# A transformer block on one core: side work of the attention stage given fixed places, a first output tile inside attention, and two units taking turns in the down projection

## The chip, the cores and the metric

The kernel runs on one core of a Trainium2 chip, in one launch. The metric is the device time of that launch in microseconds (us); several runs are made and their median is compared. A profile of one further execution gives the trace that is read below. "PE" is the matrix engine TensorE, "DVE" VectorE, "ACT" ScalarE, "POOL" GpSimd, and "SP" the sequencer that issues every DMA of this kernel.

## The reference

The block takes 4096 tokens of width 512 in float32: linear attention with 16 heads over 4 key/value heads, a residual and a layer norm, then a gated feed-forward network with Hadamard transforms, a residual and a second layer norm.

```python
q, k, v = x @ Wq.T, x @ Wk.T, x @ Wv.T          # 16 heads, 4 kv heads, head size 128
q, k = rope(q), rope(k)
qf, kf = elu(q) + 1, elu(k) + 1
# a running state over the tokens, per head
state += kf[:, None] * v[None, :];  z += kf
o = (qf @ state) / (qf @ z + 1e-6)
x = layernorm(x + o @ Wo.T)
h = fwht(x * SU_ug) / 64
h = silu(h @ W_gate.T * s_gate) * (h @ W_up.T * s_up)      # 2048 wide
x = layernorm(x + (fwht(h * SU_dp) / 64) @ W_down.T * s_down)
```

## The kernel before, in words

**Arithmetic.** Each float32 operand of a product is split in two parts of the type float32r: the high part is an ACT copy (`hi`), the low part a subtraction on DVE or POOL (`lo`); this is `hilo`, lines 88 to 90. A product is three matmuls: high by high, high by low, low by high.

**Attention** (lines 140 to 507). The key/value heads are worked in two passes of two heads; each pass goes over 16 blocks of 256 tokens. A block has four slots `(n, g, p)`: head `g`, half `p` of the block; 128 slots in all, counted by `i`. In a slot the loop traces a projection of two query heads (`proj_q`, line 314, five slots ahead of its use), parts of the next block's keys, values and state, the scores of the next slot (`scores`, 327, whose result `A` two POOL operations of line 351 mask), and the products of this slot (`av`, 354: `ps_num` and `ps_den`). The numerators go to `num_d` in DRAM; denominators go to `den_d`, and `recip` (107) turns them into reciprocals in `rec_d`.

**Side work of attention.** Weights of the second pass are loaded and split around slot 56. `wcomb` (385) forms sums of the up and gate weights that a Strassen-like product with 7 instead of 8 block products needs later: for each of eight pairs four loads, four POOL additions (line 394) and four stores to `was_d`. `load_wo` (100) loads and splits the output weights `Wo`, 14 heads from slot 118 on.

**Output projection** (624 to 773). For each of 32 token tiles `norm_o` (630) multiplies the numerators (`nt`) by the broadcast reciprocals (`rb`) and splits the result; 48 matmuls of 512 columns make the tile (`ps_wo`, line 737); two tiles are layer-normed together. Beside it run the front transform of the feed-forward input and the Hadamard transform of `W_down` (`prep_down`).

**Up and gate** (843 to 942): 32 steps of 7 products (`ps_a`, `ps_b`, `ps_c`, line 870). **Down** (992 to 1049): eight units of 512 tokens, each with the same 7 products `s` of 48 matmuls (`ps_da`, `ps_db`, `ps_dc`, line 1025). For the first unit the 7 operands of `W_down` are also loaded (`braw`) and split (`split_b`, 797); later units find them there. The activations come as `hraw` and are split by `h_split`.

**What sets the order.** The program is traced in the order of the source and then reordered engine by engine by the framework's list scheduler (`schedule_with_timeline_sim`), within what data and buffers allow; each engine then runs its own list strictly in order. `tc.keep_in_program_order` holds an instruction behind everything traced before it on its engine. All DMAs are one such list, on SP: an entry that waits holds back all that follow. Each DMA also waits for the one eight places before it, so eight are under way at most. Buffers come from rings: `praw` has 3 for raw inputs (tag `raw`), `wres` 28 tiles (24 hold the weights of a pass, so 4 are free), the pool `rp` 10 for `hraw` and `braw`.

Of the kernel before, what the change touches and what calls it, by code (L numbers as in the profile page):

```python
# [26 lines left out]
LAG = 1  # L27
# [16 lines left out]
def kernel(  # L44
# [28 lines left out]
    yq_d = [[dram.tile([128, 2, 512], F32, name=f"yq_d{f}_{k}") for k in range(7)] for f in range(4)]  # L73
    was_d = [{k: dram.tile([128, 512], F32, name=f"was_d{p}{k}") for k in ("S1", "S2", "S3", "S4")} for p in range(8)]
# [7 lines left out]

    def load_raw(src):
        raw = praw.tile([128, 512], F32, tag="raw", name="raw")
        dma(raw, src)
        return raw

    def hilo(hi, lo, src, eng=V):
        S.activation(hi, src, AF.Copy)  # L89
        eng.tensor_tensor(lo, src, hi.bitcast(F32), ALU.subtract)  # L90

    def load_w(src, pool=wres, eng=V, **kw):
        raw = load_raw(src)
        hi, lo = (pool.tile([128, 512], F32R, tag="w", name=n, **kw) for n in ("wh", "wl"))
        hilo(hi, lo, raw, eng)
        return hi, lo

    WO = []

    def load_wo(n):  # L100
        for _ in range(n):
            if len(WO) < NH - 2:
                WO.append(load_w(wo[len(WO)], eng=G if len(WO) % 2 else V))

    late = {}

    def recip(b):
        dn = pout.tile([128, 2, 16], F32, tag="dn", name="dn", bufs=2)
        for j in range(2):
            dma(dn[:, j], den_d[2 * b + j].rearrange("g h c q -> (g h c q)").rearrange("(p n) -> p n", p=128))  # L110
        V.reciprocal(dn, dn)
        for j in range(2):
            dma(rec_d[2 * b + j].rearrange("(p n) -> p n", p=128), dn[:, j])
# [3 lines left out]
    def pre_rb(t, g, pin=False):  # L117
        rb = late["p"].tile([128, 512], F32, tag="rb", name="rb", bufs=5)
        dma(rb, rec_d[t][g * 512:(g + 1) * 512].partition_broadcast(128), pin)
        cur[t]["rb"].append(rb)  # L120

    def pre(t):
        if t in (12, 16):
            recip(NB - 2 + (t == 16))
        nt = late["p"].tile([128, 16, 128], F32, tag="nt", name="nt", bufs=2)
        cur[t] = dict(nt=nt, rb=[])
        if t:
            dma(nt, num_d[t].rearrange("p g n -> p (g n)"), t < 3)
        if t < 2:
            for g in range(4):  # L130
                if t == 0:
                    dma(nt[:, 4 * g:4 * g + 4], num_d[t][:, g])
                pre_rb(t, g, t == 1 and g == 0)
        if t % 2 == 0:
            cur["yp"] = late["p"].tile([128, 2, DM], F32, tag="yp", name="yp", bufs=3)
        cur[t]["yp"] = cur["yp"]
        dma(cur["yp"][:, t % 2], x_n[t * 128:(t + 1) * 128])


    with ExitStack() as es:  # L140
# [18 lines left out]
        def weights_v(s, j):  # L159
            W["v", s, j] = load_w(wv[s, :, j * 512:(j + 1) * 512])  # L160

        def weights_k(s, g):
            W["k", s, g] = load_w(wk[2 * s + g])

        def weights_q(s, g):
            for h in range(4):
                W["q", s, g, h] = load_w(wq[8 * s + 4 * g + h])

        def load_x(n):
            b = n % NB  # L170
            hi = pe.tile([128, 4, 256], F32R, tag="xh", name="xh")
            lo = pe.tile([128, 4, 256], F32R, tag="xl", name="xl")
            hf, lf = (a.rearrange("p k t -> p (k t)") for a in (hi, lo))
            for j in range(2):
                c = slice(j * 512, (j + 1) * 512)
                if n >= NB:
                    dma(hf[:, c], xs_d[b][:, 0, c])
                    dma(lf[:, c], xs_d[b][:, 1, c])
                else:
                    hilo(hf[:, c], lf[:, c], load_raw(x_t[b, :, c]))  # L180
                    dma(xs_d[b][:, 0, c], hf[:, c])
                    dma(xs_d[b][:, 1, c], lf[:, c])
                yield
            csb = pe.tile([128, 2, 256], F32, tag="csb", name="csb")
            dma(csb, cs[b])
            blk[n] = dict(xh=hi, xl=lo, csb=csb)
# [198 lines left out]
        def wcomb(p):  # L385
            r = {}
            for it in range(2):
                for kh in range(2):
                    x = wres.tile([128, 2, 2, 128], F32, tag="w", name="wq")
                    dma(x, wug[2 * p + it].rearrange("p (u k m) -> p u k m", u=2, k=4)[:, :, 2 * kh:2 * kh + 2])  # L390
                    r[it, kh] = x
            for key, o, a, b, op in (("S3", (0, 0), (0, 0), (1, 0), ALU.subtract), ("S1", (1, 0), (1, 0), (1, 1), ALU.add),
                                     ("S2", (1, 1), (0, 0), (1, 1), ALU.subtract), ("S4", (0, 1), (0, 1), (1, 1), ALU.add)):
                G.tensor_tensor(r[o], r[a], r[b], op)
                dma(was_d[p][key], r[o].rearrange("p u k m -> p (u k m)"))
# [3 lines left out]
        NQ = len(slots)  # L399
        gx = load_x(0)  # L400
# [3 lines left out]
        dma(rowm_s, rowm)  # L404
# [3 lines left out]
        dma(idt, ident)  # L408
        dma(sel32, sel)
# [17 lines left out]
        run(load_x(1))  # L427
        run(state(0, 0))
# [6 lines left out]
        nsc = SA  # L435
        gk = gs1 = gv = None
        for i, (n, g, p) in enumerate(slots):
# [11 lines left out]
            if i == NQ - 10:  # L449
                load_wo(NH - 2)  # L450
            if i == NQ - 3:
                early.close()
                late["s"] = ExitStack()
                late["p"] = late["s"].enter_context(tc.tile_pool(name="cl", bufs=2, side="right", reuse_waits="tile"))
                pre(0)
# [44 lines left out]
            if sl == (1, 0) and 18 <= n < 26:  # L500
                wcomb(n - 18)
            if sl == (1, 1):
                if NB + LAG <= n < N - 2 + LAG:
                    recip(n - NB - LAG)
                blk.pop(n - 1, None)

        pre(1)
# [13 lines left out]
    def xtile(shape, dt, name):  # L521
        return mid.tile(list(shape), dt, tag="x4", name=name, bufs=2)
# [101 lines left out]
    with ExitStack() as es:  # L624
        p2 = es.enter_context(tc.tile_pool(name="c2", bufs=2, reuse_waits="tile"))
# [4 lines left out]
        def norm_o(t, g):  # L630
            c = cur[t]
            rb = c["rb"][g].rearrange("p (h n) -> p h n", h=4)
# [10 lines left out]
        load_wo(NH)  # L643
        for h in (NH - 2, NH - 1):
            w = xtile([128, 2, 512], F32R, "wx")
            hilo(w[:, 0], w[:, 1], load_raw(wo[h]))
            WO.append((w[:, 0], w[:, 1]))
        for g in range(KVH):
            norm_o(0, g)
# [77 lines left out]
        for t in range(32):  # L727
            if t + 2 < 32:
                pre(t + 2)
            ps = pwo.tile([128, DM], F32, tag="wo", name="ps_wo")  # L730
            i = 0
            for g in range(KVH):
                oh, ol = cur[t][g]
                for h in range(4):
                    wh, wl = WO[4 * g + h]
                    for l, r in ((oh, wh), (oh, wl), (ol, wh)):
                        T.matmul(ps, l[:, h], r, start=i == 0, stop=i == 47)  # L737
                        i += 1
                if t == 31:
                    for s in (2 * g, 2 * g + 1):  # L740
                        if s < 7:
                            asplit(0, s)
                if t + 1 < 32:
                    norm_o(t + 1, g)
                    if t + 2 < 32:
                        pre_rb(t + 2, g)
            yp = cur[t]["yp"]
            y = yp[:, t % 2]
            V.tensor_tensor(y, ps, y, ALU.add)
# [9 lines left out]
            if t >= 1:  # L759
                step(gd, 4)  # L760
# [16 lines left out]
    rp = ctx.enter_context(tc.tile_pool(name="rp", bufs=10, reuse_waits="tile"))  # L777
    BW = [None] * 7
# [33 lines left out]
    def h_split_x(s, his, los):  # L812
        HOP[0, s] = []
        for qd, raw in enumerate(HR.pop((0, s))):
            hi, lo = (x[qd // 2][:, 2 * (qd % 2):2 * (qd % 2) + 2] for x in (his, los))
            hilo(hi, lo, raw, G if qd == 3 else V)
            HOP[0, s].append((hi, lo))

    with ExitStack() as es:
# [23 lines left out]
        for n in range(NS):  # L843
# [15 lines left out]
            for s, tag in enumerate(SEQ):  # L859
# [41 lines left out]
                if p == 7:  # L901
# [4 lines left out]
                    elif s == 0:  # L906
# [3 lines left out]
                        h_load(0, 1)  # L910
# [6 lines left out]
                    elif s == 4:  # L917
                        split_b(1)
                        h_load(0, 2)
                    elif s == 6:  # L920
                        split_b(2)
                        load_b(3)
# [21 lines left out]
    with ExitStack() as es:  # L944
        pd = es.enter_context(tc.tile_pool(name="d1", bufs=2, reuse_waits="tile"))
        order = [(n, s) for n in range(len(units)) for s in range(7)]
        for n in range(1, len(units)):
# [43 lines left out]
        y_load(0)  # L991
        for idx, (n, s) in enumerate(order):
            if 0 < idx and idx + 1 < len(order):
                h_split(*order[idx + 1])
            if n == 0 and s + 3 < 7:
                split_b(s + 3)
            if 0 < idx and idx + 2 < len(order):
                h_load(*order[idx + 2])
            if n == 0 and s + 4 < 7:
                load_b(s + 4)  # L1000
# [4 lines left out]
            if s == 3 and n + 1 < len(units):  # L1005
                y_load(n + 1)
# [100 lines left out]
```

## Time and profile before

| | |
|---|---|
| median of 3 runs | 2345.06 us (2343.75 to 2345.25) |
| the profiled execution | 2340.29 us, its span 2338.2 us |
| mean granted clock of TensorE | 0.989 |
| PE busy / DVE / ACT / POOL | 2269.3 / 1812.0 / 1401.7 / 1243.7 us |
| moved by DMA | 484.16 MB, mean 207 GB/s |
| attention, first to last product | about 4.8 to 963.6 us |
| output projection | about 966 to 1360 us |
| up and gate / down | about 1360 to 2001 / 1985 to 2338 us |

The span is the time from the first to the last instruction in the trace; the execution's own time is 2.1 us longer. Rows of the timeline give start, duration, engine, source line, operation, tile written and tiles read, and in brackets the idle time of that engine just before, with what ended it. A table of windows gives, for a stretch of the span, each engine's busy time, the clock that was granted to PE, and the share and rate of the DMA engines. Matmuls are pipelined and a matmul's end is modelled, so a matmul that is issued late looks long: the distance between starts says more than the busy share.

### The profile page before, as it was taken

What the parts mean: (1) busy time and instruction counts of PE and PEld (TensorE: products, weight loads), DVE (VectorE), ACT (ScalarE), POOL (GpSimd) and SP (SyncE); (2) the same over time, 40 slices, a digit from 0 to 9 for tenths busy, and PEclk for the clock granted to TensorE, in tenths of its full rate; (3) what the DMA queues carried; (4) which work ended last, traced back from release to release, by engine and by line L of the source; (5) the groups of instructions that cost most, each with busy time, mean ns of one, the idle gap of its engine ahead of it and who ended that gap; (6) DMA issues with size and microseconds to landing.
All of it is one profiled execution on the core that took longest, in us unless ns stands there. A gap on an engine that the chain in (4) does not pass through costs nothing.

```text
span 2338.2 us, 42338 instructions
## 1 busy us (share of the span) xinstructions
PE 2269.3 (97%) x14432; PEld 2015.0 (86%) x14432; DVE 1812.0 (77%) x2812; ACT 1401.7 (60%) x2483; POOL 1243.7 (53%) x999
## 2 busy tenths in 40 slices
PE   7999999988999999899999999999999999899998
PEld 6999999987899999688878887788878888799998
DVE  7999999988898889678898776676766766665555
ACT  6777777766677777344444466655655655555553
POOL 2455454476654445367888526565565555533332
PEclk9999999999999999899999999999999999899999
DMA  6554555677744445878997977775765657867673
GB/s 186 145 152 146 161 161 155 170 214 218 213 133 129 129 135 142 279 256 269 279 294 253 312 240 217 245 254 187 227 207 188 223 189 212 285 229 249 224 248 128
DMA packets 369528, 484.16 MB, mean 207 GB/s; under 512 B 68670, under 2 KB 224384, under 8 KB 365344
## 3 DMA queue, kind: packets, MB, share of 16 engines
q1 hardware_dynamic: 369312, 481.45, 66.0%
q8 instruction: 114, 1.87, 0.3%
q14 instruction: 102, 0.84, 0.1%
HBM read 282.76 MB, written 156.76 MB: 188 GB/s over the span
## 4 chain that ended last, share of the span: by engine, by line
PE 83%; DVE 6%; DMA 5%; issue 2%; POOL 2%; ACT 1%; SPq 1%; DVEq 0%; POOLq 0%; ACTq 0%
PE ps_wo L737 15%; PE ps_a L870 15%; PE ps_qk L244 13%; PE ps_da L1025 8%; PE ps_b L870 7%; PE ps_num L371 5%; PE ps_db L1025 4%; PE ps_c L870 4%; PE ps_s L294 3%; PE ps_v L197 3%; PE ps_dc L1025 2%; PE ps_sc L337 1%; PE ps_sc L338 1%; PE ps_den L372 1%; DVE x L230 1%
## 5 line engine op out<-in xcount | busy, mean ns | idle before, releaser
L351 POOL TENSOR_SCALAR_AFFINE_SELECT A<-A 64x512 fp32r<-64x512 f32 x256 | 220.4, 861 | 286.9 <-DVE am L347 187.5
L244 PE MATMUL ps_qk<-xh,wh 128*128 128x256 f32 x1280 | 358.9, 280 | 6.3 <-DVE x L230 3.7
L244 PE MATMUL ps_qk<-xl,wh 128*128 128x256 f32 x1280 | 356.9, 279 | 0.6 <-DVE xl L90 0.6
L244 PE MATMUL ps_qk<-xh,wl 128*128 128x256 f32 x1280 | 357.1, 279 | 0.0
L90 DVE TENSOR_TENSOR wol<-A,woh 128x512 fp32r<-128x512 f32 x217 | 231.4, 1071 | 106.9 <-ACT woh L89 92.4
L852 POOL TENSOR_TENSOR cc<-cc 128x512 f32<-128x512 f32 x96 | 149.2, 1556 | 278.8 <-ACT cc L849 169.9
L226 POOL TENSOR_TENSOR sw<-sw,csb 128x512 f32<-128x512 f32 x160 | 219.7, 1374 | 141.9 <-ACT sw L225 133.8
L244 PEld LDWEIGHTS ps_qk<-xh,wh 128*128 128x128 f32 x1280 | 242.5, 189 | 8.0 <-DVE x L230 3.3
L244 PEld LDWEIGHTS ps_qk<-xl,wh 128*128 128x128 f32 x1280 | 241.7, 189 | 2.0 <-DVE xl L90 0.8
L244 PEld LDWEIGHTS ps_qk<-xh,wl 128*128 128x128 f32 x1280 | 241.7, 189 | 0.8
L89 ACT ACTIVATE woh<-A 128x512 fp32r<-128x512 f32 x217 | 135.5, 630 | 129.0 <-PE ps_b L870 75.2
L89 ACT ACTIVATE hah<-hraw 128x512 fp32r<-128x512 f32 x216 | 134.8, 630 | 129.5 <-PE ps_da L1025 68.1
L870 PE MATMUL ps_a<-yol,woh 128*128 128x512 f32 x512 | 202.5, 395 | 0.0
L90 POOL TENSOR_TENSOR hal<-hraw,hah 128x512 fp32r<-128x512 f32 x77 | 101.5, 1319 | 189.1 <-PE ps_da L1025 73.1
L870 PE MATMUL ps_a<-yoh,woh 128*128 128x512 f32 x512 | 201.9, 396 | 0.0
L870 PE MATMUL ps_a<-yoh,wol 128*128 128x512 f32 x512 | 199.4, 396 | 0.0
L90 DVE TENSOR_TENSOR hal<-hraw,hah 128x512 fp32r<-128x512 f32 x139 | 102.3, 744 | 111.7 <-PE ps_da L1025 45.7
L737 PE MATMUL ps_wo<-wh,oh 128*128 128x512 f32 x448 | 178.6, 399 | 2.8 <-ACT oh L89 2.8
L737 PE MATMUL ps_wo<-wh,ol 128*128 128x512 f32 x448 | 178.6, 399 | 0.0
L737 PE MATMUL ps_wo<-wl,oh 128*128 128x512 f32 x448 | 178.0, 397 | 0.0
L231 ACT ACTIVATE sw<-x,neg 128x512 f32<-128x512 f32 x160 | 115.5, 722 | 78.0 <-DVE x L230 75.9
L877 ACT ACTIVATE sv<-ps_a,wsc 128x512 f32<-128x512 f32 x192 | 127.2, 680 | 39.6 <-PE ps_a L870 39.5
(256 smaller groups left out, 7290.2 us busy)
## 6 DMA issues: line engine op xcount, KB each, us to landing
hraw<-hop_d SPq DMA_DIRECT2D x224, 256.0 KB
vd<-vhl SPq DMA_DIRECT2D x128, 256.0 KB
num_d<-num SPq DMA_DIRECT2D x128, 256.0 KB
rb<-rec_d SPq DMA_DIRECT2D x128, 256.0 KB
hop_d<-hS SPq DMA_DIRECT2D x128, 256.0 KB
nt<-num_d SPq DMA_DIRECT2D x31, 1024.0 KB
A<-in_wug_dram SPq DMA_DIRECT2D x93, 256.0 KB
hop_d<-cc SPq DMA_DIRECT2D x64, 256.0 KB
```

Source lines behind the costliest of these rows:

```text
L89: S.activation(hi, src, AF.Copy)
L90: eng.tensor_tensor(lo, src, hi.bitcast(F32), ALU.subtract)
L226: G.tensor_tensor(sw, sw, sinb, ALU.mult)
L231: S.activation(sw, x1, AF.Exp, bias=neg1)
L244: T.matmul(ps[:, j], W[key][wa][:, k * 128:(k + 1) * 128], B[xa][:, k], start=i == 0, stop=i == 11)
L351: G.affine_select(ah, ah.bitcast(F32), pattern=[[0, 8], [1, 64]], compare_op=ALU.is_ge, fill=0.0, base=0, channel_multiplier=-1)
L371: T.matmul(ps[:, c2], l, r, start=i == 0, stop=i == len(ops) - 1)
L737: T.matmul(ps, l[:, h], r, start=i == 0, stop=i == 47)
L852: G.tensor_tensor(x, x, c.pop(("g", q)), ALU.mult)
L870: T.matmul(ps, w[:, u, k], y[:, k], start=first and i == 0, stop=i == 5, skip_group_check=not first)
L877: S.activation(x, ps, AF.Copy, scale=sc)
L1025: T.matmul(ps[:, j], ops[qd][al][:, r, js], BW[s][bl][ip], start=first and i == 0, stop=i >= 45 or last and i == 23, skip_group_check=True)
```

## The change

The output weights, the weight sums, the first output tile and the down units change place; no arithmetic is added or removed.

1. At the start the first 14 raw tiles (inputs, `wv`, `wk`, `wq`) are all loaded ahead, into `praw` and into rings that are idle then (`num`, `s32`, `sh`, `sl`); the copies of block 0 to `xs_d` move behind block 1's load. Half of the query weights' low parts go to POOL.
2. `wcomb` becomes a generator whose pieces are pinned to slots 4 to 43 and 62 to 101, one piece in a slot, one POOL addition in two.
3. `Wo` heads 0 to 11 are loaded and split one head a slot in slots 102 to 115, stored to a new `wo_d` in DRAM, and loaded back ready split in slots 121 to 123, when weight tiles come free. Heads 12 to 15 come raw in slot 124 and are split at the end.
4. Output tile 0 is normalised in slots 116 to 126 and multiplied (`ps_w0`) within the attention block, where the scheduler may mix it with the last slots.
5. In the down stage units 0 and 1 take turns, product by product, so that a split operand of `W_down` serves two products in a row.

Reciprocals are computed a block after their load, `rb` and `yp` rings are shared between two pools of the same total, and `prep_down` starts at tile 3 instead of 1.

```diff
     def load_raw(src):
-        raw = praw.tile([128, 512], F32, tag="raw", name="raw")
+        pool, tag = first.pop(0) if first else (praw, "raw")
+        raw = pool.tile([128, 512], F32, tag=tag, name="raw")
         dma(raw, src)
         return raw
...
+    def wo_stage(h):
+        raw = praw.tile([128, 512], F32, tag="raw", name="raw")
+        dma(raw, wo[h], True)
+        yield
+        hi, lo = (wres.tile([128, 512], F32R, tag="w", name=x) for x in ("wh", "wl"))
+        hilo(hi, lo, raw, G if h % 2 else V, True)
+        yield
+        dma(wo_d[h][0], hi, True)
+        dma(wo_d[h][1], lo, True)
+
+    def wo_load(*hs):
+        for h in hs:
+            hi, lo = (wres.tile([128, 512], F32R, tag="w", name=x) for x in ("wh", "wl"))
+            dma(hi, wo_d[h][0], True)
+            dma(lo, wo_d[h][1], True)
+            WO.append((hi, lo))
...
             for key, o, a, b, op in (("S3", (0, 0), (0, 0), (1, 0), ALU.subtract), ...
-                G.tensor_tensor(r[o], r[a], r[b], op)
-                dma(was_d[p][key], r[o].rearrange("p u k m -> p (u k m)"))
+                yield
+                pin(G.tensor_tensor(r[o], r[a], r[b], op))
+                yield
+                dma(was_d[p][key], r[o].rearrange("p u k m -> p (u k m)"), True)
...
+        first.extend([(praw, "raw")] * 3 + [(p3, t) for t in ("num", "s32", "sh", "sl") for _ in range(3)])
...
-            if sl == (1, 0) and 18 <= n < 26:
-                wcomb(n - 18)
+            if 4 <= i < 44 or 62 <= i < 102:
+                go(gw)
+            elif 102 <= i < 116:
+                go(gwo)
+            elif i == 116:
+                o_load(0, *(wres.tile([128, 4, 128], F32R, tag="w", name=x) for x in ("oh0", "ol0")))
...
+            elif i == 121:
+                wo_load(0, 1, 2)
+            elif i == 122:
+                wo_load(3, 4, 5, 6, 7)
+            elif i == 123:
+                wo_load(8, 9, 10, 11)
...
+        o_split(2, V)
+        pre_rb(5)
+        o_split(3, V)
+        wo_split(G, 12, 13)
+        wo_split(V, 14)
+        wo_split(G, 15)
+        ps0 = pmm.tile([128, DM], F32, tag="mm", name="ps_w0")
+        wo_tile(0, ps0)
...
-        order = [(n, s) for n in range(len(units)) for s in range(7)]
-        for n in range(1, len(units)):
+        order = [(n, s) for s in range(7) for n in range(2)]
+        order += [(n, s) for n in range(2, len(units)) for s in range(7)]
+        for n in range(3, len(units)):
             order.remove((n, 0))
             order.insert(order.index((n - 1, 5)), (n, 0))
...
         y_load(0)
+        y_load(1)
         for idx, (n, s) in enumerate(order):
             if 0 < idx and idx + 1 < len(order):
                 h_split(*order[idx + 1])
-            if n == 0 and s + 3 < 7:
-                split_b(s + 3)
+            if n == 0 and s + 2 < 7:
+                split_b(s + 2)
```

## The prediction, made before the changed kernel was run

> **What bounds the kernel now.** I read the page, then a table of windows, then the waits, then timelines at the worst places. PE is busy for 97% of the span and carries 83% of the chain that ended last, so only PE's lost time can be won, and the matmuls stay the same in number. The windows show where it is lost: in the start, in the middle of attention, at the change to the output projection, and at the start of down. In the stretches between, PE is never idle.
>
> ```profile
> PE 83%; DVE 6%; DMA 5%; issue 2%; POOL 2%; ACT 1%; SPq 1%; DVEq 0%; POOLq 0%; ACTq 0%
> ...
> 0.00:60.00 60.00, 44.41 (x300) 41.42 (x301) 42.95 (x64) 35.65 (x59) 16.64 (x20) 0.94 0.59 181
> 400.00:680.00 280.00, 258.81 (x2028) 241.67 (x2027) 243.96 (x389) 188.57 (x337) 172.62 (x153) 0.99 0.65 192
> 932.80:982.10 49.30, 38.01 (x178) 30.20 (x176) 35.26 (x58) 21.78 (x41) 19.15 (x21) 0.79 0.85 264
> 2001.00:2031.00 30.00, 18.95 (x134) 18.45 (x133) 20.36 (x22) 12.67 (x23) 15.88 (x11) 0.77 0.87 285
> ```
>
> Columns are window, length, busy time of PE, its weight loads, DVE, ACT, POOL, then granted clock, DMA share and GB/s. To be seen: the four places, and that the granted clock falls there too. The causes stand in the waits and timelines:
>
> ```profile
> 10.48 5.52 SPq L58 DMA_DIRECT2D raw<-in_wq_dram  x4
> ...
> POOL wq L394 <- DMA wq<-in_wug_dram: 15.1, 8, 5.1
> PE ps_num L371 <- POOL A L351: 11.5, 11, 3.2
> ...
> 475.31 1.26 POOL L394 TENSOR_TENSOR wq<-wq 128x512 f32<-128x512 f32 x1 [5.21 <-issue]
> 477.35 0.51 PE L371 MATMUL ps_num<-A,vd 128*128 128x256 f32 x2 [3.21 <-POOL A L351]
> ...
> 938.61 0.63 ACT L89 ACTIVATE wh<-raw 128x512 fp32r<-128x512 f32 x1 [1.60 <-DMA raw<-in_wo_dram]
> 939.78 0.58 PE L371 MATMUL ps_num<-qh,sh 128*128 128x256 f32 x1 [3.89 <-ACT num L375]
> ...
> 2015.55 0.63 ACT L89 ACTIVATE wdzh<-braw 128x512 fp32r<-128x512 f32 x1 [4.41 <-DMA braw<-wdop_d]
> PE ps_da L1025 <- ACT hah L89: 10.5, 1, 10.5
> ```
>
> At the start, loads of raw weights wait for one of three buffers. In the middle a POOL addition of `wcomb` waits for its load, and the masks behind it in POOL's list, and so PE, wait too. At 938 an ACT copy of `Wo` waits for its DMA, and the copy that empties a PSUM bank stands behind it. In down, ACT waits for `braw` with the activations' copies behind.
>
> **What each place costs now.** A full slot of attention takes 6.975 us (the first `ps_den` of slots 13 and 25 start at 149.7 and 233.4). *Middle:* slots 47 and 85 start so at 386.9 and 683.5: 296.6 us for 38 slots, 265.1 at the full pace, so 31.5 lost, more than the 21.2 of idle, since the matmuls between waits also start late. *Start:* 300 matmuls at 0.118 us (the step between starts at full clock) are 35.4 of 60 us; 4.8 us pass before the first, so 19.8 is lost. *Change of stage:* the last `ps_qk` starts at 932.7 and the first output tile ends at 982.1. The 130 matmuls of attention in between are 15.3 us at 0.118, the tile 48 x 0.233 = 11.2: 22.9 lost. *Down:* from 2001.6 to 2027.4 run two products, 2 x 5.71: 14.4 lost. Together 88.6.
>
> **The change, part by part.**
>
> *Start.* The order of SP's list after the change has the 14 raw loads and `csb` ahead of every store; they no longer wait for buffers, only for the DMA eight places before. PE's gaps of 2.8 us (for `wv`, at 9.78) and 2.6 (for `wq`, at 28.3) go, and four `lo` parts leave DVE (4 x 0.69 = 2.8). What is late next is DVE: it is busy 39.4 of 40 us from 40 to 80. So the gain is what DVE starts earlier and is spared: about 5.4 + 2.8. I take 8; bounds 3 (the 3.9 MB at 220 GB/s come no sooner) and 13.
>
> *Middle.* POOL's list now has one addition per two slots, two slots behind its loads; 1.29 us every 13.95, on an engine busy 152 of 300 us before slot 44 and 113 of 240 after 62. The four loads, and each store, a slot after its addition, fill SP's list in even steps. Nothing of `wcomb` and `Wo` remains between slots 44 and 62. But the second pass's 24 splits stand where they stood (slots 48 and 55 to 58): they keep a loss. Slots 48 to 50 now last 8.4 and 8.8 us instead of 6.975 (3.3 lost); slots 55 to 59 last 42.7 instead of 27.9, of which the two waits for `wcomb`'s loads make 5 to 8. I leave 3.3 + 6 + 1 = 10 and take a gain of 21; bounds 12 and 29.
>
> Here a rule of the Trainium skill speaks against the change. GPSIMD Engine Reference, section 1, says that GpSimd shares its SBUF interfaces with VectorE and contends with DVE instructions that have two SBUF inputs. The trace agrees in part:
>
> ```profile
> L325 DVE TENSOR_TENSOR ql<-sw,qh 128x512 fp32r<-128x512 f32 x44 | 41.0, 931 | 5.4 <-ACT qh L323 4.9
> L230 DVE SCALAR_TENSOR_TENSOR x<-ps_qk,sw 128x512 f32<-128x512 f32 x54 | 36.6, 678 | 7.0 <-POOL sw L226 7.0
> ```
>
> Both have the same size; the one with two SBUF inputs takes 931 ns in the mean, the one that reads PSUM 678. DVE is busy 279 of 300 us in the first pass, and 16 of the 32 additions move there. If by the rule each held DVE up for its whole 1.29 us, 20.6 us would come upon 276 us, DVE would pass 100%, and some 2 us of the gain would be lost. By the rows, the stretch was 26 us over 140 POOL operations, 0.19 us each: 3 us in 276, hidden. I follow the rows. The same for the half of the `Wo` splits on POOL.
>
> *Change of stage.* Gone from it: 14 raw `Wo` loads with their splits, and the wait at 938. Added: 24 loads of 256 KB from `wo_d` instead of 14, two O operands by POOL at the end (2 x 1.3) and three `Wo` splits (3 x 1.3). 22 of the tile's 48 matmuls (5.1 us) now stand among the last slots' products in PE's list, in what were holes. With DVE, ACT and POOL free of splits, the chain of the last slots could end near 953 instead of 963.3. But the DMAs decide: behind the last block's `vd`, SP's list has 1.5 + 2.5 + 2 MB of `wo_d`, 2.25 MB of stores and `vd`, 1 MB for O, 1 MB raw `Wo`, then 1.75 MB for tile 1: 12 MB. From 932 on, at the 315 GB/s of the window 960 to 1000, the last lands at 970, the raw `Wo` near 963; split, the tile ends near 969 to 970. The skill (DMA: Bandwidth & Descriptors, Specifications) gives 358 GB/s as one core's HBM limit, by which it would be 965; no window here passes 315, so I take that. The gain is 12. Below it stands 3 (tile 1 also waits for its `rb`, in SP's list behind a load that waits for `norm_o`), above 20 (the DMA is hidden).
>
> *Down.* A split of `W_down` serves 11.4 us of matmuls instead of 5.7; in that time 3 MB must come, 263 GB/s, where the old order asked for 2 MB in 5.7, 350. The cover is thin: `y_load(1)` brings another 1 MB forward, and DVE has about ten operations of 0.7 to 1.3 us per 11.4. I leave 5 of 14.4: a gain of 9; bounds 3 and 13.
>
> *Neutral, one answer:* `recip` later, `rb` and `yp` in two pools of the same total, `prep_down` from tile 3 on. They stand in a stage where PE shows 338.7 busy of 340 and nothing idles but 1.3 us; if the DMA there (88%) slipped it would cost a few us. `wo_d`'s stores, 6.3 MB over 14 slots, lie on a DMA busy 48%.
>
> *The granted clock* is inside these sums: [...]a gap of 3.9 us at 936 to 940 also made the matmuls after it step at 0.21.
>
> Sum: 8 + 21 + 12 + 9 = 50; three new small waits that I can't name are allowed 1 us each: 47. The profiled execution of 2340.3 becomes 2293. The median of the runs stands 4.8 above it: 2298.
>
> **The rivals.**
>
> *A: the waits only move.* DMA stays the late one at both changes of stage, and DVE at the start. For it: DMA shares of 0.85 and 0.87 there, and 12.6 MB more to move. Against it: at the start and in the middle the share is 0.59 and 0.65. It would give 3 + 16 + 3 + 3 = 25: 2320.
>
> *B: SP's list holds the blocks back; slower.* Every side step is pinned on SP. A `was_d` or `wo_d` store that waits for its POOL operation, or a load that waits for a tile, keeps `num_d` stores and the next block's `vs` and `vd` behind it; `av` waits for `vd`, ACT's `num` copy for the store. It would act in 94 slots. It decides once a slot loses 0.5 us: then 47 us eat the gain. At 0.65 it gives 61 of loss, 2359. Against it: each store is traced a slot (7 us) after its operation, and the masks end 1.2 to 3.5 us ahead of their use in the slots concerned.
>
> *C: it works better than I allow:* all holes but the unavoidable close; 13 + 29 + 18 + 13 = 73: 2272.
>
> That the change does not do what it says is excluded: the list of POOL has the additions at slots 8 to 44 and 66 to 102, and PE's the new order.
>
> **How the numbers follow.** Forecast 0.66, A 0.18, C 0.08, B 0.07, no net change 0.01. The forecast's own range is 2285 to 2312; to leave out no more than 0.2 it reaches to A's middle and near C: 2280 to 2321. A difference under 0.2%, 4.7 us, is about what a measurement here can't tell from none. Faster 0.92, same 0.01, slower 0.07.
>
> **What would show it.** Right: slots of 7 us throughout 62 to 116, no POOL addition waiting for `wug`; `ps_w0` among the last `ps_num`, its end 11 us or more earlier against the last `ps_qk`; the first gap of down under 4 us. Wrong: `ps_w0` waiting for `wo_d` or raw `Wo` past 975, `ps_num` waiting for `vd` in slots with side work, DVE's mean for `ql` over 1.1 us in the first pass.

## The result, and the profile after

The median is 2346.93 us after and 2345.51 before (12 runs each). The ratio is 1.0002, 95% interval 0.9994 to 1.001: no difference. The forecast was 2298, with a range from 2280 to 2321.

The two profiled executions stand close as well: spans of 2341.2 and 2338.2 us. So the account can be made stage by stage. The page with its chain, and the four windows again (the third now from slot 121 to the end of tile 1):

```profile
span 2341.2 us, 42361 instructions
...
PE 60%; DVE 17%; DMA 9%; issue 4%; POOL 4%; ACT 4%; SPq 1%; DVEq 0%; POOLq 0%; ACTq 0%
```

```profile
0.00:60.00 60.00, 53.53 (x403) 50.43 (x404) 51.60 (x80) 44.97 (x77) 27.13 (x29) 1.00 0.70 208
400.00:680.00 280.00, 273.81 (x2201) 258.40 (x2199) 253.54 (x409) 202.54 (x360) 156.85 (x145) 0.99 0.57 161
918.10:988.90 70.80, 48.28 (x241) 37.02 (x239) 35.48 (x59) 22.84 (x42) 25.02 (x23) 0.88 0.88 287
2001.00:2031.00 30.00, 24.01 (x171) 22.85 (x170) 16.48 (x18) 12.64 (x23) 19.20 (x14) 0.89 0.90 274
```

Read first the count of PE's matmuls in the same time: 403 instead of 300 in the first 60 us, 2201 instead of 2028 from 400 to 680. There the change works. Then the chain: PE carries 60% of it, where it carried 83%, and DVE and DMA 26% instead of 11%. Waits that were off the path are now on it. The starts of the same matmuls in both traces tell where:

| stretch | forecast, us won | traces, us won |
|---|---|---|
| start to slot 13 | 8 | 7.2 |
| slots 13 to 47 | 0 | -3.8 |
| slots 47 to 85 | 21 | 23.2 |
| slots 85 to 104 | 0 | -0.4 |
| slots 104 to 117 | 0 | -8.9 |
| slot 117 to the start of tile 1 | 12 | -0.8 |
| tile 1 | 0 | -11.7 |
| tiles 2 to 30 | 0 | -0.9 |
| tile 31 and the first four steps of up and gate | 0 | -8.7 |
| rest of up and gate | 0 | -0.8 |
| down | 9 | 2.7 |
| sum | 50 | -2.9 |

One execution fixes these only so far: in e4 below, whose attention is that of the kernel before, slot 85 came 6 us later than in the trace of before. The large rows repeat, though: from its start to that of the next tile, tile 1 took 23.3 us in the changed kernel, 22.7 to 24.3 in six of its variants (e2, e3, e5, e8, e11, e12), and 11.6 before. And the kernels that have the spread sums without the staged `Wo` (e1, e9, e10) lose 3.9 to 4.5 us between slots 13 and 47 too.

The four steps are the first four of the 32 of up and gate; the expectations below call them "the first step".

The waits at the three stage changes, from the timelines after (start, duration, engine, operation, and in brackets the idle time before it and what ended it):

```profile
970.33 1.47 SPq L58 DMA_DIRECT2D rb<-rec_d  x3
...
979.97 1.30 DVE L784 TENSOR_TENSOR ps_on<-nt,rb 128x512 f32<-128x512 f32 x2 [7.61 <-DMA rb<-rec_d]
...
981.36 0.80 PE L185 MATMUL ps_wo<-wh,oh 128*128 128x512 f32 x1 [6.33 <-ACT oh L96]
...
1358.85 0.80 PE L1012 MATMUL ps_a<-yoh,woh 128*128 128x512 f32 x1 [3.27 <-DVE yp L887]
...
2017.35 0.69 DVE L1176 TENSOR_TENSOR yres<-ps_da,yres 128x512 f32<-128x512 f32 x1 [5.22 <-DMA yres<-y_d]
...
2019.53 0.58 PE L1166 MATMUL ps_dc<-wdh,hal 128*128 128x256 f32 x1 [5.09 <-DVE hal L97]
```

In tile 1, one of the three broadcast loads of reciprocals that SP issues from 970.33 on is awaited until 979.97; DVE, ACT and PE stand behind it in turn. At up and gate, the first product waits for DVE's addition of tile 31. In down, DVE waits for the residual rows `yres`, and the subtraction for `hal`, which PE needs, stands behind that wait in DVE's list.

### The profile page after: what moved, and what is told of

Its sections match the earlier page's. It is cut to its first block, busy times and chain, and to the rows that moved or that the text cites. A ratio compares the mean times of both kernels' runs of the same rounds, so it can differ in the third digit from the quotient of the medians.

```text
span 2341.2 us, 42361 instructions
## 1 busy us (share of the span) xinstructions
PE 2267.5 (97%) x14432; PEld 2007.8 (86%) x14432; DVE 1809.9 (77%) x2797; ACT 1399.7 (60%) x2483; POOL 1288.6 (55%) x1014
## 4 chain that ended last, share of the span: by engine, by line
PE 60%; DVE 17%; DMA 9%; issue 4%; POOL 4%; ACT 4%; SPq 1%; DVEq 0%; POOLq 0%; ACTq 0%
PE ps_a L1012 14%; PE ps_wo L185 11%; PE ps_da L1166 7%; PE ps_b L1012 7%; PE ps_qk L300 5%; PE ps_db L1166 4%; PE ps_c L1012 4%; DVE x L286 2%; PE ps_dc L1166 2%; PE ps_num L427 2%; DVE ps_qk L283 2%; DVE sw L290 2%; DMA rb<-rec_d 1%; PE ps_s L350 1%; DVE am L403 1%
## 5 line engine op out<-in xcount | busy, mean ns | idle before, releaser
L407 POOL TENSOR_SCALAR_AFFINE_SELECT A<-A 64x512 fp32r<-64x512 f32 x256 | 231.6, 905 | 324.4 <-DVE am L403 203.8
L97 DVE TENSOR_TENSOR wol<-A,woh 128x512 fp32r<-128x512 f32 x217 | 225.8, 1045 | 110.0 <-ACT woh L96 94.9
L282 POOL TENSOR_TENSOR sw<-sw,csb 128x512 f32<-128x512 f32 x160 | 229.3, 1436 | 71.1 <-ACT sw L281 57.0
L97 POOL TENSOR_TENSOR hal<-hraw,hah 128x512 fp32r<-128x512 f32 x78 | 106.3, 1367 | 178.9 <-PE ps_da L1166 73.1
L185 PE MATMUL ps_wo<-wh,oh 128*128 128x512 f32 x372 | 148.7, 400 | 8.0 <-ACT oh L96 8.0
L1019 ACT ACTIVATE sv<-ps_a,wsc 128x512 f32<-128x512 f32 x192 | 127.4, 681 | 40.5 <-PE ps_a L1012 40.4
L185 PE MATMUL ps_wo<-wh,ol 128*128 128x512 f32 x372 | 148.3, 399 | 1.8 <-DVE ol L97 1.8
L185 PE MATMUL ps_wo<-wl,oh 128*128 128x512 f32 x372 | 147.9, 398 | 0.0
```

What stands on the lines that cost most here:

```text
L97: j = eng.tensor_tensor(lo, src, hi.bitcast(F32), ALU.subtract)
L282: G.tensor_tensor(sw, sw, sinb, ALU.mult)
L407: G.affine_select(ah, ah.bitcast(F32), pattern=[[0, 8], [1, 64]], compare_op=ALU.is_ge, fill=0.0, base=0, channel_multiplier=-1)
L1019: S.activation(x, ps, AF.Copy, scale=sc)
```

## The experiments

The theory (P): the parts at the start and in the middle give what was forecast, and the parts that move `Wo` and its neighbours take it back at places of their own. The rival (D): the DMA sets when the output projection can run, so an earlier attention only waits longer. Times are medians, beside the kernel before on the same chip: 2344.1 us for e1 to e4, 2344.3 for e5 to e8, 2344.0 for e9 to e11, 2344.7 for e12.

**e1: parts 1 and 2 alone.**

```diff
 # before.py, with load_raw, early_raw and wcomb of the changed kernel
+            if 4 <= i < 44 or 62 <= i < 102:
+                go(gw)
-            if sl == (1, 0) and 18 <= n < 26:
-                wcomb(n - 18)
```

> The kernel before with two parts of the change alone: the early raw loads at the start, and the weight sums spread over slots 4 to 43 and 62 to 101. Nothing else is changed. Theory P (paid back later): the trace of the whole change had gained 7 us by slot 13, lost 4 in the rest of the first pass and gained 23 from slot 47 to 85; the output weights and the later stages took it back. Without those parts the 26 us stay: 2345.5 - 26 = about 2319. Rival D (the DMA sets the end of the stage): the loads at the change to the output projection end when they end, and an earlier attention only waits longer there: 2340 or more.

2326.7 us, ratio 0.9922 (0.991 to 0.9934): 17 won, and they last to the end. D falls. P's 26 came from two single traces. Of the 9 that lack, e10 finds about 7: e1's trace has waits of 12.2 us for `vs`, the changed kernel's 5.9 and e10's 4.3.

**e2: the staging of `Wo` left out** for 11 of 12 heads, the later loads kept.

```diff
-            gs = [wo_stage(h) for h in range(NH - 4)]
+            gs = [wo_stage(0)]
 # and wo_load reads wo_d[0]
```

> The changed kernel with the staging of the output weights left out for 11 of 12 heads (no raw load, no split, no store; every head is loaded from the first one's copy). The loads at the end of attention and the first tile are as in the changed kernel. Theory P: slots 104 to 117 took 99.5 us instead of 91 because the splits stand in full slots; without them 91 again, and the 9 us go through to the end: 2347 - 9 = 2338. Rival D: slots 104 to 117 get 9 us shorter as well, but the output tiles 0 and 1 wait that much longer for their DMAs: 2345 to 2347.

2334.8, ratio 0.996 (0.9948 to 0.9972): 10 to 12 less than the changed kernel (by the ratios and by the medians). Slots 104 to 117 take 93.3 us instead of 99.5, and that goes through. One split is left, head 0's; e8 comes back to it.

**e3: one tile of the PSUM ring taken first and not used.**

```diff
+        pwo.tile([128, DM], F32, tag="wo", name="ps_wo")
```

> The changed kernel with one unused tile taken from the PSUM ring of the output tiles first, so that tile 31 stands in the same bank as before (31 tiles in a ring of three had shifted it by one). Theory P: the first product of up and gate no longer waits for VectorE's last addition (3.27 us), nor runs its first 12 matmuls at half clock (2.4 us): 5 to 9 us less, 2338 to 2342. Rival F (what is left of the front transform and of the preparation of W_down, which start two tiles later, delays the first step): the gap closes but the first step still takes 88 us instead of 83: at most 3 us less, 2344.

2346.9, ratio 1.0012 (1.0003 to 1.0021). In the built program the unused tile got no bank of its own, so this is the changed kernel once more and says nothing of banks. It does say how far two measurements of one kernel lie apart: 1.0012 and 1.0002.

**e4: the order of down alone**, in the kernel before.

```diff
-        order = [(n, s) for n in range(len(units)) for s in range(7)]
+        order = [(n, s) for s in range(7) for n in range(2)]
+        order += [(n, s) for n in range(2, len(units)) for s in range(7)]
 # with the loads and splits of the changed kernel's down
```

> The kernel before with the order of down alone changed: two units take turns for the first 14 products, with the second unit's loads drawn forward. Theory P: as in the changed kernel, 3 us are won: the 10.5 us wait for W_down goes, and a wait of 5 us for an operand of the activations, with half clock after it, comes in its place; 2342. The forecast's own term: 9 us, 2336. Rival D: DMA is at 0.87 to 0.90 of its time there whatever the order: 0.

2341.6, ratio 0.9989 (0.9983 to 0.9995): 2.5 won, as P has it. The gap is there too:

```profile
2021.73 0.58 PE L1024 MATMUL ps_dc<-wdh,hal 128*128 128x256 f32 x1 [5.18 <-DVE hal L90]
```

**e5: the first `ps_a` in another bank.**

```diff
+    dummy = pgu.tile([128, 512], F32, tag="a", name="ps_x", bufs=4)
+    V.memset(dummy[:, 0:1], 0.0)
```

> The changed kernel with one VectorE write of a single column into the PSUM bank that the first product of up and gate took; in the built program this moves that product from bank 0, where output tile 31 stands, to bank 3. (The unused tile of e3 got no bank of its own, so e3 changed nothing.) Theory P: the wait of 3.3 to 3.9 us at the first product goes and so do the 12 matmuls at half clock, 2.4 us: 4 to 6 us less, 2341 to 2343. Rival F: the front transform then waits later in the step by as much: 0 to 2 us less.

2346.2, no gain: F is right. The wait at the first product is gone, but two of 1.5 us come 8 and 13 us after it, one on ACT's `woh`, and the four steps take 89.4 us (87.8 in the changed kernel, 82.5 before). The bank was where the delay showed, not its cause.

**e6: the low parts of `Wo` not loaded** at the end of attention.

```diff
-            dma(hi, wo_d[h][0], True)
-            dma(lo, wo_d[h][1], True)
-            WO.append((hi, lo))
+            dma(hi, wo_d[h][0], True)
+            WO.append((hi, hi))
```

> The changed kernel with the low parts of 12 output weights not loaded at the end of attention (their high parts stand in): 12 of 24 loads, 3 MB, are left out; the count of matmuls is the same. Theory P (bytes: at the change of stage the DMA moves hi and lo, twice the raw weights): from slot 121 to the start of output tile 1 it takes 47 us in the changed kernel, 9 us less here, and tile 1 loses nothing more: about -10, 2337. Rival L (the place in SP's list: the loads for O's last two heads are traced behind two slots and wait for them, not for bytes): tile 0 under 4 us earlier, 2343 or more.

2337.4, ratio 0.997 (0.9961 to 0.998): 8 to 10 less. From slot 121 to tile 1 it takes 40.5 us, 47.5 in the changed kernel. The wait before the last two heads' matmuls falls from 9.4 to 2.4 us. So the loads in front of them are the cause: `hi` and `lo` are twice the raw weights. Whether their bytes or their number counts is not separated, since the edit halves both.

**e7: three broadcast loads of tile 1 left out.**

```diff
+        if 5 <= k < 8:
+            RB[k] = RB[4]
```

> The changed kernel with three of tile 1's four broadcast loads of reciprocals (g = 1 to 3) left out; the first one's stands in for them. Theory P: output tile 1, which takes 23.3 us instead of 11.4, waits for these loads (the last was issued at 970 and came at 980); without them 12 to 15 us: 8 to 11 less, 2337. Rival L: something else in the same queue (the numerators of tile 2, the transform constants) is late then: 3 us or less.

2337.1, ratio 0.9969 (0.9959 to 0.998): 8 to 10 less. Tile 1 takes 17.3 us, a wait of 3.2 remains. In this trace the loads are 6.0 of the 11.7 us that tile 1 lost. Why they come so late was not tested: the loads ahead of them are one candidate, and another is the `rb` ring in two pools, since two of the three stand in the second pool.

**e8: the splits left out, their DMAs kept.**

```diff
-        hi, lo = (wres.tile([128, 512], F32R, tag="w", name=x) for x in ("wh", "wl"))
-        hilo(hi, lo, raw, G if h % 2 else V, True)
         yield
-        dma(wo_d[h][0], hi, True)
-        dma(wo_d[h][1], lo, True)
+        dma(wo_d[h][0], raw, True)
+        dma(wo_d[h][1], raw, True)
```

> The changed kernel with the 12 splits of output weights in slots 102 to 116 left out but all of their DMAs kept (raw tiles are stored twice). Theory P (engines): slots 104 to 117 took 99.5 us, 93.3 with the whole staging left out; the splits fill DVE and POOL, so about 93 here too, and the total like that of e2: about 2336. Rival D (their 9 MB of DMA in SP's list): 98 to 100, the total unchanged at 2345 to 2347.

2331.9, ratio 0.9945 (0.9933 to 0.9957): 13 to 15 less. Slots 104 to 117 in the windows, first after, then here (window, length, busy time of PE, weight loads, DVE, ACT, POOL, clock, DMA share, GB/s):

```profile
790.20:889.70 99.50, 93.73 (x750) 87.69 (x748) 92.33 (x144) 73.26 (x130) 59.37 (x50) 1.00 0.70 212
```

```profile
791.40:881.90 90.50, 90.50 (x750) 86.66 (x748) 79.71 (x139) 66.09 (x119) 47.83 (x43) 1.00 0.77 232
```

The same 750 matmuls run at the full pace of 6.96 us a slot with all the DMA present, so it is not the DMA. DVE has 12.6 us less to do, though only five of its instructions are gone, and the whole stretch is 9 us shorter.

Why is this faster than e2, which leaves the DMAs out as well? From slot 106 to 117 both take 76.6 us. The difference is in slots 104 and 105, 16.7 us in e2 and 13.9 here, and there e2 has the one split it kept:

```profile
789.28 0.63 ACT L96 ACTIVATE wh<-raw 128x512 fp32r<-128x512 f32 x1 [3.98 <-DMA raw<-in_wo_dram]
789.95 0.69 DVE L97 TENSOR_TENSOR wl<-raw,wh 128x512 fp32r<-128x512 f32 x1 [3.62 <-ACT wh L96]
```

Its two operations last 1.3 us together; ACT and DVE first stand still for it, 4.0 and 3.6 us, and the two slots grow by 2.8. In the changed kernel ACT waits 3.7 us for the same split, and the two slots take 17.4: 3.6 of the 9 us are there.

**e9: e1 with the later reciprocals.**

```diff
-                    recip(n - NB - LAG)
+                    cur["dn"] = recip_load(n - NB - LAG)
 # and V.reciprocal four slots on, pinned
```

> e1 (early raw loads and spread weight sums alone) with the changed kernel's later reciprocals added: the denominators are loaded four slots before VectorE takes their reciprocals, which are pinned. e1 had gained 12.7 us by slot 104, kernels with the whole change 19 to 26. Theory R (in e1 VectorE waits for the denominators' load, 2.4 us in four waits, in slots that have no slack left): by slot 104 about 24 us, total about 2317. Rival V (the difference is when the state's operand vs lands behind the loads for the weight sums, at slots 72 to 76 and 92 to 100, and differs by list order): 2324 to 2327, as in e1.

2326.2 against 2326.7 for e1: nothing that can be measured, and R falls. "Neutral" was right for this edit. By slot 104 the trace is 19.9 us ahead, between the two theories.

**e10: e9 with halved bursts, the first range two slots later, and the new order of down.**

```diff
                     r[it, kh] = x
-            yield
+                yield
...
-            if 4 <= i < 44 or 62 <= i < 102:
+            if 6 <= i < 46 or 62 <= i < 102:
```

> e9 with two more edits: the four loads of a weight sum split over two slots and the first range moved from slot 4 to 6 (6 to 45), and the turn-taking order of down from the change. Theory V: slots 4 and 72 lose 6 and 2 to 6 us in all kernels with spread sums because vs lands behind 1 MB of loads in SP's list; with half of it at a time most of that goes: 6 to 9 us less than e9, and 2.5 less for down: 2308 to 2316. If the loads are not the cause: 2.5 less than e9.

2316.7, ratio 0.9886 (0.9871 to 0.9901): the fastest here, 27 below before. Its reason is in e1's trace, SP's list first, then PE:

```profile
569.87 2.57 SPq L58 DMA_DIRECT2D wsum<-in_wug_dram  x4
572.48 3.87 SPq L58 DMA_DIRECT2D vd<-vhl  x4
576.39 1.87 SPq L58 DMA_DIRECT2D vs<-v  x2
...
585.97 1.49 PE L306 MATMUL ps_s<-vs,kfn 64*128 64x128 f32 x4 [5.18 <-DMA vs<-v]
```

The 1 MB for one weight sum is issued just ahead of the block's `vd` and `vs`, and PE waits for `vs`. The changed kernel has the same wait at 87 (3.3 us) and 579 (2.6 us). In e10 the first is gone and slots 0 to 6 take 46.3 us, 51.3 after; the second is still 2.0. The total is 9.5 below e9, of which down should be 2.5. The halving and the later start are not separated.

**e11: the preparation of `W_down` from tile 1 again.**

```diff
-            if t >= 3:
+            if t >= 1:
                 step(gd, 4)
```

> The changed kernel with the preparation of W_down started at output tile 1 again instead of 3. Theory G: from the start of tile 31 to the second step of up and gate it takes 102 us in the changed kernel and 93.7 before, because the later preparation pushes the front transform's last stores back by 11 us in SP's list; undone, 94 to 96: about 2339. Rival S (the moved reciprocal loads and the split rings of rb and yp do it): stays at 101 to 103, total 2345 to 2347.

2339.2, ratio 0.9979 (0.9968 to 0.9989): 5 to 8 below the changed kernel. From the start of tile 31 to the end of the first four steps of up and gate it takes 94.6 us, close to before (93.7), not 102.5. SP's stores of the last layer norm and the next step's weights behind them come earlier, first after, then here:

```profile
1345.89 5.51 SPq L58 DMA_DIRECT2D yraw<-yq_d  x4
1364.35 1.03 SPq L58 DMA_DIRECT2D y_d<-yp  x2
```

```profile
1345.04 0.43 SPq L58 DMA_DIRECT2D yraw<-yq_d  x1
1360.82 1.02 SPq L58 DMA_DIRECT2D y_d<-yp  x2
```

Tile 31 starts at 1344.2 after and at 1345.3 here, so `y_d` is stored 20 and 15.5 us later. After, four of the seven inputs of up and gate are still to load when tile 31 begins; splits of such inputs stand ahead of its addition in DVE's list.

**e12: all low parts of the staged `Wo` on VectorE.**

```diff
-        hilo(hi, lo, raw, G if h % 2 else V, True)
+        hilo(hi, lo, raw, V, True)
```

> The changed kernel with the low parts of all 12 staged output weights formed by VectorE; half of them were POOL's. Theory C (while POOL subtracts, VectorE's operations with two SBUF inputs are held up for about as long: in slots 104 to 117 the mean for ql is 1180 ns, 830 without the splits): six POOL operations cost VectorE about 6 x 1.3 = 7.8 us and six more subtractions cost it 6 x 0.69 = 4.1, so VectorE gains 3.7 us: slots 104 to 117 take 96, not 99.5, ql's mean falls to about 850, the total is 3 to 4 lower, 2343. Rival W (the splits cost by their own time alone; moving six to the fuller engine costs 4.1): 103 us, 2350.

2349.7, ratio 1.0026 (1.0015 to 1.0037): 3 to 6 more, and slots 104 to 117 take 101.9. C is wrong: with none of these splits on POOL, `ql` is still at 1097 ns. The numbers of W nearly came (103 and 2350), but a wait appears that neither theory had (us in total, times, longest):

```profile
DVE wl L97 <- ACT wh L96: 8.4, 5, 3.9
ACT wh L96 <- DMA raw<-in_wo_dram: 8.1, 5, 2.2
```

A pinned split waits in ACT's and DVE's lists for its raw tile, with the slot's own work behind it. In the changed kernel ACT waits so for 4.0 us in these slots, and for 3.7 just ahead of them. That the splits cost these slots 9 us is shown by e8, and that 2.8 of it can come from one late split by e2. How the rest divides between DVE's own time, its stretch beside POOL, and the pinned wait is open.

## Why the prediction was wrong

*Right.* The start (8 forecast, 7.2 found) and the middle (21, 23.2), and e1 shows that they are real in the total, at 17 of the 29 forecast; that the two rows come so close to the forecast is in part luck of two single traces. That pinned loads can hold a block back in SP's list was rival B's mechanism. It acts at slots 4 and 72, not in 94 of them: there e10 won part of about 7 us.

*Wrong: "hidden" in full slots.* The step put the additions at 3 us and called them hidden on a DVE at 93%, and then: "The same for the half of the `Wo` splits on POOL." That is no cover. The first pass lost 3.8 us between slots 13 and 47, the splits 9 in slots 104 to 117 and 13 to 15 in the total. The rule of the Trainium skill that spoke against the change (GPSIMD Engine Reference, section 1) was set aside for its size; here is its form, slots 13 to 47, before and after (count, busy us, mean ns of one, idle time before):

```profile
L325 DVE TENSOR_TENSOR ql<-sw,qh 128x512 fp32r<-128x512 f32 x34 | 30.7, 903 | 4.6 <-ACT qh L323 4.2
L230 DVE SCALAR_TENSOR_TENSOR x<-ps_qk,sw 128x512 f32<-128x512 f32 x42 | 28.5, 678 | 5.8 <-POOL sw L226 5.8
L90 DVE TENSOR_TENSOR xl<-raw,xh 128x512 fp32r<-128x512 f32 x18 | 16.8, 972 | 0.0
```

```profile
L381 DVE TENSOR_TENSOR ql<-sw,qh 128x512 fp32r<-128x512 f32 x34 | 33.0, 971 | 3.2 <-ACT qh L379 2.8
L286 DVE SCALAR_TENSOR_TENSOR x<-ps_qk,sw 128x512 f32<-128x512 f32 x42 | 28.6, 682 | 7.7 <-POOL sw L282 7.7
L97 DVE TENSOR_TENSOR xl<-raw,xh 128x512 fp32r<-128x512 f32 x18 | 21.2, 1218 | 0.0
```

Of the three rows, the two with two SBUF inputs grew, `ql` from 903 to 971 ns and `xl` from 972 to 1218; the one that reads PSUM did not. That agrees with the rule in kind, though one row with two SBUF inputs (`sl`) fell, from 816 to 759. DVE's busy time rose from 218 to 223 us for 12 additions, about 0.4 each, twice the row taken. The failing step was not the 0.2 but the word "hidden". That the additions themselves cost the 3.8 us is argued from these rows: no run takes them out and keeps their DMAs. And e2 and e12 warn against putting all of the splits' cost on POOL.

*Wrong: the change of stage.* From slot 117 to tile 1 nothing was won where 12 stood. The DMA rate was right (315 estimated; 318 GB/s in the window 932.8 to 982.1), and tile 0 did end 43 us after the last `ps_qk` instead of 49; but slots 117 and later lost that again. What the sum left out was tile 1. Its `rb` loads were named only as a lower bound; the tile lost 11.7 us, and e7 gives 8 to 10 back. Staged weights move 6 MB in place of 3 MB in the one stage that waits for DMA: e6 gives 8 to 10 us back.

*Wrong: "neutral".* `prep_down` two tiles later cost 5 to 8 us (e11). It was judged by the stage that it stands in, where PE was always busy, not by what ends last at its end. The later reciprocals were neutral, as said (e9).

*Mis-sized: down.* 9 forecast, 2.5 measured (e4). The wait for `braw` did go. The forecast named the 1 MB of `y_load(1)` as a risk to the DMA; it struck DVE's list, where `yres` stands ahead of `hal`.

The sum assumed that a stage's gain lasts if nothing new is named, and allowed 3 us for what it could not name. Rival A (waits only move, 2320) had the kind right but kept 25. In the traces 33 us were won and 36 given back, 33 of these in four stretches. Of the signs named ahead, the slots were not at 7 us throughout, tile 0 ended 6 us earlier against the last `ps_qk` and not 11, and the first gap of down was 5.1 us and not under 4; `ql` stayed under 1.1 us in the first pass, so that bound was set too high to warn.

## What to carry to other kernels

Side work spread over slots is free only where the engine that it uses, and each list it stands in, has slack in those slots; here an engine with an average busy share of 93% had none. A load pinned ahead of a block's own loads, or a wait pinned ahead of a block's own operations, stops everything behind it, so look at what follows in SP's, ACT's and DVE's lists. Test the parts alone: here parts 1, 2 and 5 were worth 27 us with a small repair (e10), and the rest took it back.

## What the runs showed of the hardware

DMA rates of single slices: the line below gives 40 equal slices of 925 to 966 us in the changed kernel. From 934 to 942, while the split weights were loaded in 256 KB transfers, it shows 360 to 408 GB/s; the peak of 460 comes at 959, behind loads of raw `Wo`, numerators and a broadcast that rereads one row. That is above the 315 that the forecast took from longer windows, and above the 358 that the Trainium skill gives as one core's HBM limit (DMA: Bandwidth & Descriptors, Specifications), which that row works out as half of what two cores share; here one core ran. The mean over 925 to 966 was 312, so the estimate from the longer window was the useful one.

```profile
GB/s 208 286 211 168 235 378 206 270 352 404 406 408 378 404 368 360 378 256 234 374 394 376 347 205 262 96 258 368 240 208 366 410 408 460 404 394 364 394 223 29
```
